# A slot table summed on two halves of TensorE, and the later expert tiles queued behind tile 0

## The chip, the cores and the metric

The kernel runs on one NeuronCore of a Trainium2 chip: TensorE (PE, with its weight loads shown as PEld), VectorE (DVE), ScalarE (ACT), GpSimd (POOL), SyncE (SP) and the DMA engines. The metric is the device time of one launch in microseconds; a time is the median of several executions.

## The reference, cut to what matters

The input `x` is 2 x 128 x 56 x 56 in fp32. Four layers each add their output to `x` after a normalisation: agent attention, a 3x3 convolution, a mixture of experts on 2x2 patches, and a two-way Mamba layer. The change is in the third:

```python
xp = patches of x                        # 1568 tokens of 512 numbers
probs = softmax(xp @ router_w)           # 8 experts
topv, topi = top_k(probs, 2)             # weights of the two, divided by their sum
for e in range(8):
    val, g = split(xp @ w1[e], 2)        # w1[e]: 512 x 2048
    out += gate[:, e] * ((val * sigmoid(g)) @ w2[e])   # w2[e]: 1024 x 512
```

## The kernel before, in words

The kernel does only the two chosen experts of each token. The 3136 choices (14 blocks of 112 tokens, two choices each) are sorted by expert into tiles of 128 slots, so that one tile belongs to one expert. There are at least 25 tiles (`self.fewest`); a `Switch` at the end runs the few more that the routing needs.

`PatchExperts.route` makes the plan. For each choice DVE computes tile and place in the tile. A table then has to say, for each tile (column) and each slot (row), which token sits there (`whom`) and with which weight (`share`). The table is a sum of 28 fp32 matmuls on PE, one for each block and choice (L1275): the stationary operand is `is_slot[:, t, :]`, 112 x 128, one where a token has that slot; the moving operand is `what[:, t]`, 112 x 64: 32 columns of token numbers, 32 of weights. All 28 add into one PSUM tile `inv` of 128 x 64, from which DVE copies `whom` (L1284) and `share` (L1286). The operands of the first choice lie in a buffer `room0` and those of the second in `room1`. These borrow one of the two buffers of the second weights (`w2`) and one of the two of the first weights (`w1`), so the second pair of weight reads waits until the last table matmul is done.

`PatchExperts.run` does the tiles. For a tile `j`:

- `expert(j)` loads the tile's expert number from SBUF into registers on SP (L1307), for the address of the reads;
- `up_weights` (L1314, 4 MB) and `down_weights` (L1319, 2 MB) read the expert's weights on SP's DMA queue, with two buffers each;
- `gather(j)` reads the tile's 128 token rows from DRAM with an indirect DMA on POOL (L1289), into one of four buffers `xr`;
- `up` transposes the rows on PE (four matmuls, L1331), copies them on DVE (L1333), makes 64 matmuls (L1342), a sigmoid on ACT (L1351) and a product on DVE (L1353);
- `down` of the tile before makes eight matmuls (L1359); ACT multiplies by the share (L1361) and writes the result to DRAM.

The program fixes the data and the order of the text; the order on each engine is made by a scheduler that puts work where its inputs are expected to be ready. In the program before, PE has the transposes of tiles 0 to 3 in front of tile 0's first L1342, and SP has thirteen expert numbers (L1307) in front of the first weight read.

fp32 matmuls stand in the trace as two records each.

Of the kernel before, what the change touches and what calls it, by code (L numbers as in the profile page):

```python
# [8 lines left out]
F32 = mybir.dt.float32  # L9
# [8 lines left out]
P = 128  # L18
# [995 lines left out]
class PatchExperts:  # L1014
# [15 lines left out]
    def route(self, dram, wpool, conv):  # L1030
# [9 lines left out]
        with tc.tile_pool(name="l2_route", bufs=1) as one, tc.tile_pool(  # L1040
# [10 lines left out]
            nc.gpsimd.dma_start(rw[:, :, :experts], a["L2_conv_router_w"].rearrange("(c q) e -> c q e", q=4))  # L1051
            four = one.tile([P, 32], F32, name="four")
            nc.vector.tensor_reduce(four, net.ident.rearrange("p (q e) -> p e q", q=4), AX.X, ALU.add)
            shape = [T, nt, experts]

            rank = one.tile([T, experts], F32, name="rank")
# [173 lines left out]


            self.slots = []
            inv = ps.tile([P, 512], F32, name="inv", tag="tr")
            rooms = [
                wpool.tile([P, self.hidden // P, 512], F32, name="room0", tag="w2").rearrange("p j d -> p (j d)"),
                wpool.tile([P, 4, 2 * self.hidden], F32, name="room1", tag="w1").rearrange("p q f -> p (q f)"),
# [1 line left out]
            for n, room in enumerate(rooms):  # L1238
                is_slot = room[:T, : nt * SLOTS].rearrange("t (n s) -> t n s", s=SLOTS)
                what = room[:T, nt * SLOTS : nt * (SLOTS + 2 * TILES)].rearrange("t (n h j) -> t n h j", h=2, j=TILES)  # L1240
                nc.vector.tensor_tensor(hots[n], hots[n], slot, ALU.mult)
                at = one.tile([T, nt], F32, name=f"at{n}")
                nc.vector.tensor_reduce(at, hots[n], AX.X, ALU.add)
                at_i = keep.tile([T, nt], I32, name=f"at_i{n}")
                nc.vector.tensor_copy(at_i, at)
                self.slots.append(at_i)
                tile_i = one.tile([T, nt], I32, name=f"tile_i{n}")
                nc.vector.tensor_single_scalar(tile_i, at_i, 7, ALU.logical_shift_right)
                tile_f = one.tile([T, nt], F32, name=f"tile_f{n}")
                nc.vector.tensor_copy(tile_f, tile_i)  # L1250
                low = one.tile([T, nt], F32, name=f"low{n}")
                nc.vector.scalar_tensor_tensor(low, tile_f, -float(SLOTS), at, ALU.mult, ALU.add)
                by_tile = [T, nt, TILES]
                nc.vector.tensor_tensor(
                    what[:, :, 0, :],
                    count_to[:T].unsqueeze(1).to_broadcast(by_tile),
                    tile_f.unsqueeze(2).to_broadcast(by_tile),
                    ALU.is_equal,
                )
                nc.vector.tensor_tensor(  # L1260
                    what[:, :, 1, :], what[:, :, 0, :], share[n].unsqueeze(2).to_broadcast(by_tile), ALU.mult
                )
                nc.vector.tensor_tensor(
                    what[:, :, 0, :], what[:, :, 0, :], token.unsqueeze(2).to_broadcast(by_tile), ALU.mult
                )
                for some in (range(per), range(per, nt)):
                    ts = slice(some[0], some[-1] + 1)
                    nc.vector.tensor_tensor(
                        is_slot[:, ts, :],
                        slot_of.unsqueeze(1).to_broadcast([T, per, SLOTS]),  # L1270
                        low[:, ts].unsqueeze(2).to_broadcast([T, per, SLOTS]),
                        ALU.is_equal,
                    )
                    for t in some:
                        nc.tensor.matmul(  # L1275
                            inv[:, : 2 * TILES],
                            is_slot[:, t, :],
                            what[:, t].rearrange("t h j -> t (h j)"),
                            start=n == 0 and t == 0,
                            stop=n == 1 and t == nt - 1,  # L1280
                        )

            self.whom = keep.tile([P, TILES], I32, name="whom")
            nc.vector.tensor_copy(self.whom, inv[:, :TILES])  # L1284
            self.share = keep.tile([P, TILES], F32, name="share")
# [12 lines left out]
    def run(self, wpool, work, ps):  # L1298
        net, nc, a = self.net, self.net.nc, self.net.a
        experts, hidden, toks = self.experts, self.hidden, self.toks  # L1300
        nj = hidden // P

        w1s = a["L2_conv_w1"].rearrange("e (c q) f -> e c q f", q=4)
        w2s = a["L2_conv_w2"].rearrange("e (j k) d -> e k j d", k=P)

        def expert(j):
            return bass.ds(nc.sync.value_load(self.whose[0:1, j : j + 1], min_val=0, max_val=experts - 1), 1)  # L1307

        ups = [wpool.tile([P, 4, 2 * hidden], F32, name="w1", tag="w1") for _ in range(2)]
        downs = [wpool.tile([P, nj, 512], F32, name="w2", tag="w2") for _ in range(2)]  # L1310

        def up_weights(j, e):
            w1 = ups[j % 2]
            nc.sync.dma_start(w1, w1s[e].rearrange("o c q f -> (o c) q f"))  # L1314
            return w1

        def down_weights(j, e):
            w2 = downs[j % 2]
            nc.sync.dma_start(w2, w2s[e].rearrange("o k j d -> (o k) j d"))  # L1319
            return w2  # L1320

        def gather(j):
            xr = work.tile([SLOTS, 512], F32, name="xr", tag="xr", bufs=4)
            self.rows_of(xr, self.xd, self.whom[:, j : j + 1], toks)
            return xr

        def up(j, w1, xr):

            tp = ps.tile([P, 512], F32, name="xr_ps", tag="tr")
            for q in range(4):  # L1330
                nc.tensor.transpose(tp[:, q * P : (q + 1) * P], xr[:, q * P : (q + 1) * P], net.ident)  # L1331
            xc = work.tile([P, 4, SLOTS], F32, name="xs_c", tag="xs_c")
            nc.vector.tensor_copy(xc.rearrange("c q s -> c (q s)"), tp)  # L1333
            ht = work.tile([P, nj, SLOTS], F32, name="ht", tag="ht")
            for c in range(2):
                parts = []
                for part in (1, 0):
                    h_ps = ps.tile([P, 512], F32, name="h_ps", tag="h", bufs=4)
                    for i in range(4):
                        f0 = part * hidden + (4 * c + i) * P  # L1340
                        for q in range(4):
                            nc.tensor.matmul(  # L1342
                                h_ps[:, i * SLOTS : (i + 1) * SLOTS],
                                w1[:, q, f0 : f0 + P],
                                xc[:, q, :],
                                start=q == 0,
                                stop=q == 3,
                            )
                    parts.append(h_ps)
                sg = work.tile([P, 4 * SLOTS], F32, name="sg", tag="sg")  # L1350
                nc.scalar.activation(sg, parts[0], AF.Sigmoid)  # L1351
                to = ht[:, 4 * c : 4 * c + 4, :].rearrange("k j s -> k (j s)")
                nc.vector.tensor_mul(to, parts[1], sg)  # L1353
            return ht

        def down(j, ht, w2):
            o_ps = ps.tile([P, 512], F32, name="o_ps", tag="o")
            for i in range(nj):
                nc.tensor.matmul(o_ps, ht[:, i, :], w2[:, i, :], start=i == 0, stop=i == nj - 1)  # L1359
            ot = work.tile([SLOTS, 512], F32, name="ot", tag="ot")  # L1360
            nc.scalar.mul(ot, o_ps, self.share[:, j : j + 1])  # L1361
            nc.scalar.dma_start(self.os[j * SLOTS : (j + 1) * SLOTS, :], ot)


        more = nc.values_load(self.more[0:1, 0:1], min_val=0, max_val=TILES - self.fewest)
        last = None
        for j in range(self.fewest):
            e = expert(j)
            w1, w2 = up_weights(j, e), down_weights(j, e)
            ht = up(j, w1, gather(j))  # L1370
            if last is not None:
                down(*last)
            last = (j, ht, w2)
        e0 = expert(self.fewest)
        first = up_weights(self.fewest, e0), down_weights(self.fewest, e0)
        xrs = {j: gather(j) for j in range(self.fewest, self.fewest + 3)}
        before = last
        for n in net.tc.Switch(more, TILES - self.fewest + 1):
            last = before
            for j in range(self.fewest, self.fewest + n):  # L1380
                if j == self.fewest:
                    w1, w2 = first
                else:
                    e = expert(j)
                    w1, w2 = up_weights(j, e), down_weights(j, e)
                ht = up(j, w1, xrs[j] if j in xrs else gather(j))
                down(*last)
                last = (j, ht, w2)
            down(*last)
# [759 lines left out]
```

## Time and profile before

| what | value |
|---|---|
| median of three timed runs | 3039.38 us (3038.12 to 3041.95) |
| the profiled execution, its own time | 3034.5 us |
| its span, first to last instruction | 3032.4 us |
| PE busy, share of the span | 2681.1 us (88%) |
| DVE busy | 2182.4 us (72%) |
| ACT busy | 1848.6 us (61%) |
| POOL busy | 1472.2 us (49%) |
| mean granted TensorE clock | 0.945 |
| L1342 (first expert product), PE | 407.4 us in 3584 records |
| L1359 (second expert product), PE | 201.2 us in 448 records |
| idle of POOL before L1289 | 519.0 us, 474.4 of it ended by PE `xr_ps` L1331 |

How to read it: busy times of engines overlap, so they do not add up to the span. A row `line engine op out<-in xcount | busy, mean ns | idle before <-releaser` names the line of the kernel, the engine, what is written and read, the count, and which event ended the idle time before. In the timeline a row is start, duration, engine, line, operands, count, and in brackets the idle time before it and what ended it. In a table of stretches each engine has its busy time and, in brackets, the number of its records; the last columns are the granted clock of TensorE as a share of full speed, the busy share of the DMA engines, and what they moved. SPq is the queue of SyncE.

### The profile page before, as it was taken

To read this page: it belongs to the slowest core of one execution; us is meant where nothing else is said; L and a number is where in the kernel's file an instruction comes from. 1 tells how busy PE (TensorE), PEld (TensorE's weight loads), DVE (VectorE), ACT (ScalarE), POOL (GpSimd) and SP (SyncE) were. 2 spreads that over 40 slices of the span, in tenths; PEclk is the share of its full clock that TensorE was granted. 3 is DMA by queue.
4 is the path that set the end of the run, shared out by engine and by line. 5 is a ranking of instruction groups with operands and counts; after the bars stand their busy time and mean duration, and the time that the engine had idled before them with its cause. 6 is when DMAs were issued, how large, how long until landed. Compare 5 with 4: busy or idle time off the path is not lost. (4 is left out here: it accounts for less than half of the span.)

```text
span 3032.4 us, 39344 instructions
## 1 busy us (share of the span) xinstructions
PE 2681.1 (88%) x14924; PEld 1275.2 (42%) x14924; DVE 2182.4 (72%) x1845; ACT 1848.6 (61%) x2942; POOL 1472.2 (49%) x801
## 2 busy tenths in 40 slices
PE   7999999999998799999997678888888888888874
PEld 3333333333335688787875323333323333233321
DVE  5978998999886300100101599999999999999996
ACT  5778788788751100000000488888888888888884
POOL 3000010010422100000001689999999999999995
PEclk9999999999999799999998899999998999999987
DMA  1000000000002768787874555566555565545560
GB/s 55 1 1 1 1 1 1 1 1 1 1 1 60 271 266 327 302 323 308 316 309 165 133 122 113 120 141 137 118 117 117 113 147 123 126 115 118 123 142 29
DMA packets 157931, 369.29 MB, mean 122 GB/s; under 512 B 25156, under 2 KB 114980, under 8 KB 154132
## 3 DMA queue, kind: packets, MB, share of 16 engines
q1 hardware_dynamic: 135744, 339.30, 38.7%
q0 software_dynamic: 5520, 15.62, 1.7%
q10 hardware_dynamic: 16452, 11.61, 1.2%
q8 instruction: 121, 1.98, 0.3%
q14 instruction: 94, 0.77, 0.1%
HBM read 297.89 MB, written 17.20 MB: 104 GB/s over the span
## 5 line engine op out<-in xcount | busy, mean ns | idle before, releaser
L1840 POOL TENSOR_TENSOR dBu<-dtu,Bs 128x896 f32<-128x896 f32 x448 | 943.1, 2150 | 18.0 <-DMA dtu<-sp_u 16.0
L1859 DVE TENSOR_TENSOR_SCAN h<-dA,dBu 128x896 f32<-128x896 f32 x448 | 883.9, 2009 | 28.9 <-ACT dA L1829 21.3
L620 ACT ACTIVATE ex<-sc 128x896 f32<-128x896 f32 (+1 forms) x700 | 602.6, 918 | 125.0 <-PE sc L617 113.7
L1881 PE MATMUL y<-h,both 128*64 128x448 f32 x1792 | 467.5, 614 | 99.5 <-POOL h L1868 93.5
L627 DVE TENSOR_TENSOR ex_sum<-ex_sum,ex 128x1792 f32<-128x1792 f32 (+1 forms) x238 | 492.5, 2069 | 35.3 <-ACT ex L620 21.3
L1342 PEld LDWEIGHTS h_ps<-xs_c,w 128*128 128x128 f32 x3584 | 403.7, 192 | 19.6 <-ACT ot L1361 17.7
L1342 PE MATMUL h_ps<-xs_c,w 128*128 128x128 f32 x3584 | 407.4, 276 | 0.0
L617 PE MATMUL sc<-q,k 32*128 32x448 f32 (+1 forms) x2800 | 403.8, 588 | 3.6 <-ACT ex L620 2.9
L1870 DVE TENSOR_TENSOR h<-h,c_ps 128x1792 f32<-128x1792 f32 (+1 forms) x168 | 326.5, 1944 | 31.9 <-ACT c_ps L1847 14.9
L1353 DVE TENSOR_TENSOR ht<-h_ps,sg 128x512 f32<-128x512 f32 x56 | 38.5, 691 | 418.0 <-PE h_ps L1342 365.8
L635 PE MATMUL av<-ex,va 128*32 128x448 f32 (+1 forms) x2800 | 334.4, 552 | 0.1
L582 POOL TENSOR_TENSOR a_e<-a_e,a_inv 112x784 f32<-112x784 f32 x14 | 41.6, 2973 | 584.1 <-ACT ex L620 394.5
L1829 ACT ACTIVATE dA<-dt,f_A 128x448 f32<-128x448 f32 x448 | 282.8, 636 | 57.1 <-DVE h L1859 41.2
L1829 ACT ACTIVATE dA<-dt,b_A 128x448 f32<-128x448 f32 x448 | 282.7, 635 | 30.0 <-DVE h L1859 21.2
L1289 POOL DMA_INDIRECT xr<-xd,whom x28 | 28.1, 1003 | 519.0 <-PE xr_ps L1331 474.4
L1881 PEld LDWEIGHTS y<-h,both 128*64 128x64 f32 x1792 | 119.1, 148 | 371.1 <-issue 208.9
L1868 POOL TENSOR_TENSOR h<-h,Cs 128x1792 f32<-128x1792 f32 (+1 forms) x70 | 253.3, 3619 | 2.9 <-PE sp_ps L1794 1.9
L617 PEld LDWEIGHTS sc<-q,k 32*128 32x128 f32 (+1 forms) x2800 | 137.8, 181 | 230.1 <-issue 132.5
L1351 ACT ACTIVATE sg<-h_ps 128x512 f32<-128x512 f32 x56 | 33.4, 597 | 308.8 <-PE h_ps L1342 301.5
L1359 PE MATMUL o_ps<-w,ht 128*128 128x512 f32 x448 | 201.2, 593 | 1.2 <-DVE ht L1353 1.2
L1361 ACT ACTIVATE ot<-o_ps,share 128x512 f32<-128x512 f32 x28 | 19.2, 687 | 244.0 <-PE o_ps L1359 244.0
L625 DVE TENSOR_TENSOR ex_sum<-ex 128x1792 f32<-128x1792 f32 x56 | 114.4, 2042 | 54.6 <-ACT ex L620 54.5
(332 smaller groups left out, 2980.9 us busy)
## 6 DMA issues: line engine op xcount, KB each, us to landing
w<-in_L_conv_w_dram SPq DMA_DIRECT2D x28, 4096.0 KB, 20.4
w<-in_L_conv_w_dram SPq DMA_DIRECT2D x28, 2048.0 KB, 10.7
Bs<-far SPq DMA_DIRECT2D x56, 896.0 KB, 8.0
Cs<-far SPq DMA_DIRECT2D x448, 112.0 KB, 3.0
dtu<-sp_u SPq DMA_DIRECT2D x108, 224.0 KB, 3.9
dt<-dt SPq DMA_DIRECT2D x108, 224.0 KB, 5.1
os<-ot ACTq DMA_DIRECT2D x28, 256.0 KB, 7.9
xd<-xt SPq DMA_DIRECT2D x14, 224.0 KB, 2.7
```

The costliest lines, as they stand in the source:

```text
L617: nc.tensor.matmul(sc[:size, j, :BLK], self.m.k[rows, at : at + size], self.q[rows, :], start=True, stop=True)
L620: nc.scalar.activation(ex[:size, 2 * g : 2 * g + 2, :], sc[:size, :, :BLK], AF.Exp, scale=scale)
L627: nc.vector.tensor_add(self.total[g][:size], self.total[g][:size], ex[:size])
L635: nc.tensor.matmul(self.av[rows, :BLK], self.m.va[:size, i, rows], self.ex[i][:size, h, :], start=i == 0, stop=i == STEPS - 1,)
L1342: nc.tensor.matmul(h_ps[:, i * SLOTS : (i + 1) * SLOTS], w1[:, q, f0 : f0 + P], xc[:, q, :], start=q == 0, stop=q == 3,)
L1359: nc.tensor.matmul(o_ps, ht[:, i, :], w2[:, i, :], start=i == 0, stop=i == nj - 1)
L1829: nc.scalar.activation(self.dA[u][:, r * BLK : (r + 1) * BLK], self.dt2[:, m, r, :], AF.Exp, scale=self.w.A[:, j, 2 * m + r : 2 * m + r + 1],)
L1840: nc.gpsimd.tensor_tensor(self.dBu[u], self.dtu2[:, m], self.B[:, j, :].unsqueeze(1).to_broadcast(shape), ALU.mult)
L1859: nc.vector.tensor_tensor_scan(hf, af, bf, 0.0, ALU.mult, ALU.add)
L1868: nc.gpsimd.tensor_tensor(h4, h4, self.C[j].unsqueeze(1).to_broadcast(shape), ALU.mult)
L1870: nc.vector.tensor_tensor(h4, h4, self.c_ps[:, :BLK].unsqueeze(1).to_broadcast(shape), ALU.mult)
L1881: nc.tensor.matmul(self.y[r * H : (r + 1) * H, m, :BLK], both, self.hc[j][:, m, r, :], start=False, stop=j == PAIRS - 1)
```

## The change

Two things are changed.

The slot table is summed the other way round. `what[:, t]` (64 columns) becomes the stationary operand and `is_slot[:, t, :]` (128 columns) streams. The result is the transposed table, 64 x 128. Blocks with an even number write it to PSUM partitions 0 to 63 and those with an odd number to 64 to 127, so each half of the array's columns has its own sum. One DVE copy (`table`) and one more matmul against `fold`, two identity blocks on top of each other, add the two halves and turn the table back; `whom` and `share` are copied as before. `fold` is made once by a DVE add.

In `run`, tiles 1 to 3 put whatever they have on PE in queue behind tile 0's first L1342 matmul, and each tile from 1 on puts what it has on SP (number loads, weight reads) behind an earlier `w1` read: tile 1 behind tile 0's, all later ones behind tile 1's. `issue_after` orders the queue only; it adds no wait for the other instruction's end. In the built program PE then has four transposes ahead of tile 0's L1342; the transposes of tiles 1, 2 and 3 each come after the L1342 group of the tile before. SP has two number loads ahead of the first weight read, one each ahead of the `w1` reads of tiles 1 and 2 and of the `w2` read of tile 2, and seven and six ahead of the `w2` reads of tiles 3 and 4. The order of ACT and POOL is the same.

```diff
+            fold = one.tile([P, 2 * TILES], F32, name="fold")
+            nc.vector.tensor_add(fold, net.ident[:, : P // 2], net.ident[:, P // 2 :])
...
-            inv = ps.tile([P, 512], F32, name="inv", tag="tr")
+            turned = ps.tile([P, 512], F32, name="turned", tag="tr")
...
                     for t in some:
+                        g = t % 2 * 2 * TILES
                         nc.tensor.matmul(
-                            inv[:, : 2 * TILES],
+                            turned[g : g + 2 * TILES, :SLOTS],
+                            what[:, t].rearrange("t h j -> t (h j)"),
                             is_slot[:, t, :],
-                            what[:, t].rearrange("t h j -> t (h j)"),
-                            start=n == 0 and t == 0,
-                            stop=n == 1 and t == nt - 1,
+                            start=n == 0 and t < 2,
+                            stop=n == 1 and t >= nt - 2,
                         )
 
+            table = one.tile([P, SLOTS], F32, name="table")
+            nc.vector.tensor_copy(table, turned[:, :SLOTS])
+            inv = ps.tile([P, 512], F32, name="inv", tag="tr")
+            nc.tensor.matmul(inv[:, : 2 * TILES], table, fold, start=True, stop=True)
...
+        starts, fetches = [], []
+
         def up_weights(j, e):
             w1 = ups[j % 2]
-            nc.sync.dma_start(w1, w1s[e].rearrange("o c q f -> (o c) q f"))
+            dma = nc.sync.dma_start(w1, w1s[e].rearrange("o c q f -> (o c) q f"))
+            fetches.append(dma.ins)
             return w1
...
-                            nc.tensor.matmul(
+                            mm = nc.tensor.matmul(
                                 h_ps[:, i * SLOTS : (i + 1) * SLOTS],
...
+                            starts.append(mm.ins)
...
         for j in range(self.fewest):
-            e = expert(j)
-            w1, w2 = up_weights(j, e), down_weights(j, e)
-            ht = up(j, w1, gather(j))
+            behind = ExitStack()
+            if 0 < j < 4:
+                behind.enter_context(net.tc.issue_after(starts[0]))
+            if j > 0:
+                behind.enter_context(net.tc.issue_after(fetches[min(j - 1, 1)]))
+            with behind:
+                e = expert(j)
+                w1, w2 = up_weights(j, e), down_weights(j, e)
+                ht = up(j, w1, gather(j))
             if last is not None:
                 down(*last)
             last = (j, ht, w2)
```

## The prediction

> **What bounds the kernel now.** I read the page's busy slices first (40 slices of 75.8 us), then busy time and clock by stretch, then the timeline of the hand-over from routing to experts.
>
> ```profile
> PE   7999999999998799999997678888888888888874
> DVE  5978998999886300100101599999999999999996
> ```
>
> Three regimes: attention and convolution (to slice 12), a stretch where only PE is full (slices 14 to 20, the experts), and the Mamba layer, where DVE and POOL are full. The change lies at the start of the second.
>
> ```profile
> core 0: us, PE busy (x) PEld busy (x) DVE busy (x) ACT busy (x) POOL busy (x), PEclk, DMA share, GB/s
> 1012.27:1015.68 3.41, 3.41 (x18) 3.41 (x18) 1.13 (x4) 0.00 (x0) 0.00 (x0) 0.50 1.08 384
> ...
> 1022.50:1025.90 3.40, 0.00 (x0) 0.00 (x0) 0.00 (x0) 0.00 (x0) 2.48 (x4) 0.50 0.88 309
> 1029.34:1032.75 3.41, 2.51 (x11) 1.74 (x10) 1.38 (x2) 0.00 (x0) 1.77 (x2) 0.50 1.17 458
> 1032.75:1036.16 3.41, 3.38 (x17) 3.00 (x16) 0.00 (x0) 0.00 (x0) 2.22 (x3) 0.50 0.98 422
> 1036.17:1039.00 2.83, 2.83 (x27) 2.83 (x27) 0.00 (x0) 0.08 (x1) 0.00 (x0) 1.00 1.01 424
> ...
> 1114.32:1592.70 478.38, 478.36 (x3252) 387.45 (x3252) 44.95 (x65) 40.70 (x65) 19.39 (x20) 1.00 0.80 313
> ```
>
> The last row decides what a saved microsecond is worth: from tile 4 to the last tiles PE is busy 478.36 of 478.38 us, so whatever tile 4 starts earlier, the whole rest starts earlier. The other rows show the hand-over: TensorE is idle at 1022 to 1026, and granted half its clock until 1036.16.
>
> ```profile
> 1008.87 12.18 PE L1275 MATMUL inv<-room 112*128 112x64 f32 x56 [3.29 <-DVE tile_f L1250]
> 1011.35 0.38 SPq L1314 DMA_DIRECT2D w<-in_L_conv_w_dram  x1
> 1021.08 0.19 DVE L1284 CAST whom<-inv 128x32 int32<-128x32 f32 x1 [7.62 <-PE inv L1275]
> 1021.56 1.13 POOL L1289 DMA_INDIRECT xr<-xd,whom  x1 [39.58 <-DVE share L1286]
> 1029.06 1.09 PE L1331 MATMUL xr_ps<-ident,xr 128*128 128x128 f32 x4 [8.01 <-DMA xr<-xd,whom]
> 1030.59 1.11 PE L1331 MATMUL xr_ps<-ident,xr 128*128 128x128 f32 x4 [0.45 <-DMA xr<-xd,whom]
> 1032.15 2.21 PE L1331 MATMUL xr_ps<-ident,xr 128*128 128x128 f32 x8 [0.45 <-DMA xr<-xd,whom]
> 1034.15 15.42 PE L1342 MATMUL h_ps<-xs_c,w 128*128 128x128 f32 x128
> ```
>
> This is the path: slot table (28 fp32 matmuls, each two records), `whom`, first gather, transposes of tiles 0 to 3 one after another as their gathers land, then tile 0's first product. The first weights, read at 1011.35, landed after 12.3 us, at 1023.7: not what is waited for.
>
> **What the Trainium skill says.** "TensorEngine Tiling (Array Packing)", Performance Considerations, advises swapping stationary and streaming operands plus 2x column tiling when the right-hand side is 64 wide or less. That is this edit, and the trace agrees that two 64-column halves run at once:
>
> ```profile
> L1881 PE MATMUL y<-h,both 128*64 128x448 f32 x8 | 1.7, 552 | 1.8 <-POOL h L1868 1.8
> ```
>
> Eight records of 448 columns in 1.7 us; whole-array L1359 steps every 0.44 us at 512 columns (16 records in 7.03), so eight of 448 would take 3.1 in a row. "TensorE: Matmul & The Clock Gate", Part 1, says the clock is halved after an idle window of about 3.4 us and restored after a busy one, in free-running windows. The trace agrees: the half-clock span 1005.4 to 1036.16 is nine times 3.41 us. It also shows that `inv`, busy throughout, did not restore the clock, while the stretch 1032.75 to 1036.16, full of transposes and L1342, did. "DMA: Bandwidth & Descriptors", Queues, rings and completion order, says each DMA engine takes turns between queues packet by packet. The gathers agree that the neighbour matters:
>
> ```profile
> xr<-xd,whom POOLq DMA_INDIRECT x1, 7.4
> ...
> xr<-xd,whom POOLq DMA_INDIRECT x1, 12.5
> ...
> g<-os,at_i POOLq DMA_INDIRECT x1, 3.3
> ```
>
> These are issue-to-landing times: 7.4 us for the gather of 1021.56, beside the 2 MB read `w2` (1011.99 to 1033.0); 12.5 us for that of 1030.41, mostly beside the 4 MB read `w1`; 3.3 us for one of the combine stage, beside no weights.
>
> **The change, part by part.**
>
> Slot table. A half-clock `inv` record takes 12.18/56 = 0.217 us, as long as an L1342 record at half clock (0.113 doubled) although only 64 columns stream: the 128-column weight load sets it (PEld 3.41 of 3.41). Afterwards 64 columns are loaded, 128 stream, and records of two halves overlap: 14 steps of about 0.215 per choice instead of 28. The second choice's operands come from DVE at 1012.69 (L1263). So: start 1008.87, 14 steps to 1011.9, wait, restart 1012.83, 14 steps and 0.2 drain: 1016.05 against 1021.05, -5.0. If the denser stream restores the clock by then, 14 steps of 0.113: 1014.6, -6.4. I give that one chance in three, as the gap at 1012 breaks most windows.
>
> The fold then adds a PSUM copy 128x128 (0.28, row L142), 0.03 of hand-over, and one matmul between two DVE steps: 0.63 for `tot` (L1172 ends 999.21, L1179 starts 999.84), 0.8 at half clock. Together 1.1, or 0.95. `whom` moves by -3.9 (cold) or -5.5 (warm), mean -4.4. `fold` itself is one DVE add of 0.2 (row L1522, same shape) at 913 us between small DVE steps; I charge 0.1, range 0 to 0.2.
>
> Order on PE. From landing of gather 0 (1028.92) to L1342 (1034.15) are 5.2 us. With tile 0's transposes alone: 0.13 hand-over, 1.09 transposes, 0.09 and 0.69 for L1333, 0.2 to L1342: 2.2, so -3.0. Twelve transposes come back later at full clock, 3 x 0.435 (1112.89 to 1113.32 for four): +1.3. Tile 1's copy L1333 hides under four L1359 products (4 x 0.86); tiles 2 and 3 have one product as cover, as tile 4 has already, with 0.14 left open: +0.3. Net -1.4. Gathers 5 to 7, formerly issued by 1035, now wait on POOL for transposes of tiles 1 to 3 (from 1043 on); they are needed from about 1130. Nothing else is queued behind them there.
>
> Clock. Tile 0 took 15.42 against 14.45 for later tiles: 0.97 lost in 2.0 cold microseconds, since the sixteen transposes had filled the window. Now PE idles about 8 us, does 1 us of transposes, waits 1 us, and must fill a window with L1342 itself. By the rows above, 2.51 busy of 3.41 was not enough and 3.38 was; taking 2.6 as the least, that is 2.6 to 6.0 us cold, mean 4.3, half of it lost: 2.15. Net +1.2 (0.3 to 2.0).
>
> Expert reads. SP had to load thirteen expert numbers ahead of the first read:
>
> ```profile
> L1307 SPq TENSOR_LOAD <-whose_i x13: 262/262/275, 1003.1 to 1009.9; - x13
> ```
>
> Pitch 6.8/12 = 0.56 us. Now two stand ahead: first `w1` 11 x 0.56 = 6.2 earlier, issued 1005.15, landing 1017.4. This earns nothing by itself (needed at 1027; unchanged it would land at 1023.7, still 3 us of cover). The second `w1` waits for the last slot-table matmul, which frees its buffer: 1016 instead of 1021.08. Until it lands, the remaining `w2`, four gathers and itself (about 7.3 MB) pass at some 0.39 MB/us (rows above: 309 to 458 GB/s): 1036; tile 1 asks at 1046. The moved loads (seven ahead of the fourth `w2`, 3.9 us) run while SP would wait for PE anyway: reads L1319 come 21 us apart.
>
> Gather 0. Issued 0.48 after `whom` starts, 1017.7 or 1016.0. Price taken: 7.4, since `w2` is again in flight (from about 1016 to 1026). Bounds 3.3 and 12.5; I add 0.2 for overrun.
>
> Sum at tile 4: -4.4 - 1.4 + 1.2 + 0.1 + 0.2 = **-4.3 us**. The profiled execution took 3034.5 (span 3032.4), so 3030.2 there. The timed runs stand 4.9 higher (median 3039.38); none of the steps depends on that, so 3035.1. About 0.2% (6.1 us) is what a measurement of this kernel can tell from no change; the forecast gain is below that.
>
> **The rivals.**
> 1. *The gather meets `w1` instead of `w2`* (ends slower). Because reads begin 6.2 us earlier and the table only 4 to 5, `w2` may be through before gather 0 moves; it then runs beside 4 MB of `w1`. For: 12.5 to 13.1 us for gathers 4 to 7. Against: at 1017.7 `w2` has only just begun, and needed 9.3 us beside gathers (1023.7 to 1033). Price +5.1: +0.8, 3040.2. From 11.7 us of landing time on, the gain is gone.
> 2. *The halves do not overlap*: 28 steps a choice as before, plus 1.1 for the fold. `whom` +1.1, total about +1.2, 3040.6. Against: L1881.
> 3. *More than forecast*: the table warms the clock (-5.5), tile 0 warms no later than before (1.2 back), and the gather needs 6.5: -5.5 - 1.4 + 0.1 - 0.9 = -7.7, 3031.7. For: windows may fall well; against: it takes all three.
>
> **How the numbers follow.** Forecast 0.68, rival 1 0.12, rival 2 0.06, rival 3 0.14. The forecast's own spread, cold to warm table and clock 0.3 to 2.0, is -6.5 to -2.5. The range 3031.0 to 3039.5 takes in rival 3 and the better half of rivals 1 and 2. Faster by over 0.2% needs below 3033.3: rival 3 and a quarter of the forecast, 0.31. Slower by over 0.2% is only a tail of rivals 1 and 2: 0.04. Same: 0.65.
>
> **What would show it.** Right: `turned` busy about 7 us instead of 12.2, its end near 1016; `whom` near 1017; first gather landing after 7 to 8 us; four, not sixteen, transposes ahead of L1342 at 1027; half clock to 1030 or 1031; tile 4 starting 4 to 5 us earlier, and the same shift at 1592. Wrong: `turned` still 12 us, a first gather over 9 us, L1342 idle for a `w` read, or a shift at tile 4 that is gone at the end.

## The result and the profile after

| | before | after |
|---|---|---|
| median of 20 runs | 3038.86 us (3034.71 to 3044.11) | 3033.20 us (3029.39 to 3048.44) |
| ratio of the medians, 95% interval | | 0.9983 (0.9975 to 0.9992) |
| the profiled execution, its own time | 3034.5 us | 3033.72 us |
| its span | 3032.4 us | 3031.7 us |
| PE busy | 2681.1 us | 2676.5 us |

The change gains some 5 us (by the interval 2.4 to 7.6). The spans of the two profiled executions show almost none of it, and the first thing to learn from the profile is why. The timeline of the hand-over, with the columns as before (the lines of the kernel have moved: the table is L1278, L1287 and L1289, the gather L1296, the transposes L1341, the first product L1352, its weight reads L1323 and L1329):

```profile
1004.69 0.37 SPq L1323 DMA_DIRECT2D w<-in_L_conv_w_dram  x1
1008.83 3.26 PE L1278 MATMUL turned<-room 112*64 112x128 f32 x28 [3.29 <-DVE tile_f L1252]
1012.70 1.75 PE L1278 MATMUL turned<-room 112*64 112x128 f32 x28 [0.62 <-DVE room L1265]
1014.50 0.29 DVE L1287 COPY table<-turned 128x128 f32<-128x128 f32 x1 [1.07 <-PE turned L1278]
1014.84 0.43 PE L1289 MATMUL inv<-fold,table 128*128 128x64 f32 x2 [0.39 <-DVE table L1287]
1015.32 0.19 DVE L1291 CAST whom<-inv 128x32 int32<-128x32 f32 x1 [0.53 <-PE inv L1289]
1015.80 1.13 POOL L1296 DMA_INDIRECT xr<-xd,whom  x1 [33.88 <-DVE share L1293]
1022.37 1.09 PE L1341 MATMUL xr_ps<-ident,xr 128*128 128x128 f32 x4 [7.09 <-DMA xr<-xd,whom]
1024.30 16.96 PE L1352 MATMUL h_ps<-xs_c,w 128*128 128x128 f32 x128 [0.84 <-DVE xs_c L1343]
1041.10 0.60 PE L1341 MATMUL xr_ps<-ident,xr 128*128 128x128 f32 x4
```

The reader sees each step of the change: the table in two bursts of 3.26 and 1.75 us where it was one of 12.18; copy and fold; `whom` 6.49 us after the first table matmul, formerly 12.21; one group of four transposes ahead of L1352, the next only behind it at 1041.10. Tile 0 starts 9.85 us earlier but takes 16.96 us instead of 15.42. By stretch of time, in the same columns as before:

```profile
1008.89:1012.31 3.42, 3.19 (x28) 2.79 (x28) 3.42 (x7) 0.00 (x0) 0.00 (x0) 0.50 0.98 422
1012.31:1015.72 3.41, 2.18 (x30) 1.81 (x30) 1.62 (x7) 0.00 (x0) 0.00 (x0) 1.00 1.09 461
1015.72:1019.13 3.41, 0.00 (x0) 0.00 (x0) 0.00 (x0) 0.00 (x0) 2.73 (x3) 1.00 0.85 321
1019.13:1022.55 3.42, 0.18 (x1) 0.21 (x2) 0.00 (x0) 0.00 (x0) 1.42 (x2) 0.50 1.07 367
1022.55:1025.96 3.41, 2.57 (x12) 2.17 (x12) 0.69 (x1) 0.00 (x0) 1.00 (x1) 0.50 1.10 410
1025.96:1029.37 3.41, 3.41 (x18) 3.41 (x18) 0.00 (x0) 0.00 (x0) 0.00 (x0) 0.50 1.07 455
1107.74:1586.20 478.46, 478.43 (x3252) 387.52 (x3252) 44.98 (x65) 40.70 (x65) 19.38 (x20) 1.00 0.80 313
```

The first row is one window of the clock in which the new table kept TensorE busy 3.19 us; after it the clock is full (second row) and the second choice runs at full speed. The idle third row costs the clock again, from 1019.13 to 1029.37. The last row is the yardstick of the prediction: tile 4 to the last tiles, 478.46 us, formerly 478.38 (the window after ends 0.08 us later, behind the start of the same transposes). Tile 4 started at 1114.32 and now starts at 1107.74, **6.58 us earlier**, and the combine stage's first gather moves by the same (1648.74 to 1642.18).

From there to the end of the span stand 1383.7 us before and 1389.5 us after, with the same instructions (PE 3704 records, DVE 806, in both). That stage took anything from 1378.5 to 1392.6 us in the thirteen profiles of this study, and in no order that follows the edits. So 5.8 of the 6.6 us won are hidden in this one pair of executions by a stage that differs for no reason shown here; only the medians show them.

The busy slices of the page:

```profile
PE   7999999999998799999996788888888888888874
DVE  5978998999887301010102589999999999999996
```

The hand-over lies in slice 13 (7 for PE in both kernels): 6 us of 75.8 are no whole digit there. What shows is the end of the experts in slice 21, where PE falls from 7 to 6, and the start of the Mamba layer in slices 22 and 23, where it rises from 6 and 7 to 7 and 8: everything there comes a little earlier.

### The profile page after: what moved, and what is told of

Its sections match the earlier page's. It is cut to its first block, busy times and chain, and to the rows that moved or that the text cites. A ratio compares the mean times of both kernels' runs of the same rounds, so it can differ in the third digit from the quotient of the medians.

```text
span 3031.7 us, 39354 instructions
## 1 busy us (share of the span) xinstructions
PE 2676.5 (88%) x14926; PEld 1269.6 (42%) x14926; DVE 2184.8 (72%) x1847; ACT 1849.2 (61%) x2942; POOL 1471.9 (49%) x801
## 3 DMA queue, kind: packets, MB, share of 16 engines
HBM read 297.89 MB, written 17.20 MB: 104 GB/s over the span
## 5 line engine op out<-in xcount | busy, mean ns | idle before, releaser
L1352 PEld LDWEIGHTS h_ps<-xs_c,w 128*128 128x128 f32 x3584 | 404.9, 193 | 21.5 <-ACT ot L1372 19.3
L1352 PE MATMUL h_ps<-xs_c,w 128*128 128x128 f32 x3584 | 409.1, 276 | 0.9 <-DVE xs_c L1343 0.8
L1296 POOL DMA_INDIRECT xr<-xd,whom x28 | 28.1, 1003 | 512.5 <-PE xr_ps L1341 474.9
```

What stands on the lines that cost most here:

```text
L1352: mm = nc.tensor.matmul(h_ps[:, i * SLOTS : (i + 1) * SLOTS], w1[:, q, f0 : f0 + P], xc[:, q, :], start=q == 0, stop=q == 3,)
```

## The experiments

Times of the end spread by some 15 us from run to run; the steps of the hand-over spread far less. There is one profile of each kernel, but steps that several kernels share can be compared: `whom` comes out within 0.02 us, and gather 0 within 0.6 us where the reads before it are the same (6.57, 6.82 and 7.16 in the changed kernel, e11 and e7). All runs are therefore read by the **distance from the first table matmul to tile 4's first product**: before 105.45 us, after 98.91. It may stand for the end, because from tile 4 to the first gather of the combine stage there are 534.36 to 534.44 us in all thirteen profiles. `whom` and "gather 0" are counted from the first table matmul and from the issue of the first gather (to its transposes on PE).

| kernel | table | PE order | SP order | whom | gather 0 | tile 0 takes | tile 4 | ratio to before (95%) |
|---|---|---|---|---|---|---|---|---|
| before | old | old | old | 12.21 | 7.50 | 15.42 | 105.45 | 1 |
| e1 | new | old | old | 6.49 | 8.61 | 15.51 | 102.05 | 0.9985 (0.9977 to 0.9993) |
| e3 | old | new | old | 12.22 | 7.13 | 17.20 | 105.44 | 1.0000 (0.9991 to 1.0009) |
| e4 | old | old | new | 12.22 | 12.35 | 15.85 | 111.80 | 1.0021 (1.0013 to 1.0029) |
| e2 | old | new | new | 12.22 | 12.63 | 16.21 | 109.94 | 1.0016 (1.0004 to 1.0028) |
| e9 | new | new | old | 6.48 | 8.65 | 15.98 | 100.00 | 0.9988 (0.9981 to 0.9996) |
| e11 | new | old | new | 6.49 | 6.82 | 15.89 | 108.24 | 1.0009 (0.9998 to 1.0020) |
| after | new | new | new | 6.49 | 6.57 | 16.96 | 98.91 | 0.9983 (0.9975 to 0.9992) |
| e5 | one half | new | new | 8.82 | 12.20 | 16.41 | 106.11 | 1.0003 (0.9992 to 1.0014) |
| e6 | new | new | new, `w2` first | 6.50 | 10.46 | 16.75 | 102.60 | 0.9986 (0.9978 to 0.9994) |
| e7 | new | new | new, PE kept busy | 6.49 | 7.16 | 14.56 | 96.63 | 0.9967 (0.9953 to 0.9981) |
| e8 | new | new | new, reads held | 6.49 | 3.54 | 16.72 | 95.64 | 0.9969 (0.9958 to 0.9980) |
| e10 | new | new | both of these | 6.49 | 3.58 | 14.56 | 92.96 | 0.9966 (0.9959 to 0.9973) |

The first eight rows are all combinations of the three parts. The gain or loss by the distance lies within the interval of the ratio in every row (of e10, at its edge). The parts do not add: table -3.40, PE order -0.01 and SP order +6.35 make +2.94, and together they give -6.54. Of the pairs, table and SP order come near their sum (+2.79 for +2.95, e11); the other two do not (-5.45 for -3.41, e9; +4.49 for +6.34, e2).

**e1, the table alone.** The changed kernel without both orders:

```diff
-            behind = ExitStack()
-            if 0 < j < 4:
-                behind.enter_context(net.tc.issue_after(starts[0]))
-            if j > 0:
-                behind.enter_context(net.tc.issue_after(fetches[min(j - 1, 1)]))
...
```

> Only the slot table is changed; the queues of PE and SP stay as before (sixteen transposes ahead of tile 0, thirteen number loads ahead of the first weight read). Both theories: the table ends near 1015.3 and the first gather is issued near 1015.8. Theory A, the parts add up (the sum of the prediction): the gather lands after 7.4 us, at 1023.2, the four transpose groups follow as before, tile 0's first product starts near 1028.5 and tile 4 near 1108.7, 5.6 earlier than before (1114.3). Theory B, the neighbour on the DMA engines decides: the first w1 read is still issued at 1011.3 and in flight until 1023.7, so the gather runs beside 4 MB of w1 and takes 12 to 13 us; it lands at 1028 or later, and the gain of the table is mostly gone: tile 4 between 1112 and 1116. Whole time: A -5 us, B within 2 us of before.

`whom` comes 5.7 us earlier, as in the changed kernel, but tile 4 only 3.40, between the values named. The first gather now takes 8.48 us to land, and those behind it 9.4 to 9.8: with the reads where they were, `w1` is in flight until 1024.58, while they run.

**e3, the PE order alone**, on the old table and the old reads:

```diff
             behind = ExitStack()
             if 0 < j < 4:
                 behind.enter_context(net.tc.issue_after(starts[0]))
```

> Only the PE order: tile 0's transposes alone ahead of its products; table and SP order as before. The gather meets w2 as before in both theories and lands after 7.4 us at 1028.9. Tile 0's first product then starts near 1031.1 instead of 1034.15 (-3.0); twelve transposes and two open copies come back (+1.6); the clock is cold longer, since nothing fills PE before tile 0 (tile 0 17.0 instead of 15.4: +1.5). Tile 4 between 1113.6 and 1114.8, whole time within 1 us of before. If the cold clock cost nothing, tile 4 would start at 1112.7.

Tile 0 starts 21.76 us after the table's first matmul instead of 25.28, so 3.5 are won; and from there to tile 4 it takes 83.68 instead of 80.17, so 3.5 are given back: tile 0 takes 17.20 us, 1.78 more, because the sixteen transposes no longer warm the clock for it, and the other 1.7 are the twelve transposes that come back between later products.

**e4, the SP order alone, and e2, both orders**, on the old table. e4 keeps only

```diff
             if j > 0:
                 behind.enter_context(net.tc.issue_after(fetches[min(j - 1, 1)]))
```

and e2 this and the line of e3.

> Only the SP order: two number loads ahead of the first weight read; table and PE order as before, so tile 0 waits for all four gathers. Theory A (reads that come earlier earn and cost nothing): gathers 7.4 to 7.7 us, tile 4 at 1114.3, no change. Theory B: w2 is through by 1023, the four gathers run beside the second w1 read; gathers 0 to 3 take 10 to 17 us (in the changed kernel the third and fourth took 14.1 and 17.2), the fourth lands near 1040, and tile 4 starts 5 to 9 us later than before; the whole is slower by as much.

> The table is summed as before; both queue orders (PE and SP) are those of the changed kernel. The table ends at 1021.05 and the first gather is issued at 1021.5. w1 and w2 of tile 0 start near 1004.7 and are through by about 1023. Theory A (parts add up): gather 7.4 us, tile 4 moves by -3.0 + 1.6 + 1.2 to 1.5 for the colder clock: 1114.1 to 1114.5, no change. Theory B (the neighbour decides): w2 is through when the gather moves, so it runs beside the second w1 read, takes 10 to 13 us, and tile 4 starts 3 to 6 us later than before, 1117 to 1120: slower in the whole by as much.

Both are slower, by 6.35 and 4.49 us at tile 4. The timeline of e2:

```profile
1005.64 0.42 SPq L1322 DMA_DIRECT2D w<-in_L_conv_w_dram  x1
...
1021.36 0.35 SPq L1316 DMA_DIRECT2D w<-in_L_conv_w_dram  x1
1021.85 1.13 POOL L1289 DMA_INDIRECT xr<-xd,whom  x1 [39.57 <-DVE share L1286]
...
1034.48 1.09 PE L1334 MATMUL xr_ps<-ident,xr 128*128 128x128 f32 x4 [13.15 <-DMA xr<-xd,whom]
```

and the DMA issues of e2, with the time to landing last (that `w2` with its `w1` of 1005.02, then the gather of 1021.85):

```profile
w<-in_L_conv_w_dram SPq DMA_DIRECT2D x1, 4096.0 KB, 12.2
w<-in_L_conv_w_dram SPq DMA_DIRECT2D x1, 2048.0 KB, 17.1
...
xr<-xd,whom POOLq DMA_INDIRECT x1, 12.5
```

`w2`, issued at 1005.64, is through 17.1 us later, at 1022.8, when the gather has only begun; the next 4 MB `w1` is queued from 1021.36. The gather runs beside it and needs 12.5 us. This is rival 1, with its mechanism and its price (+5.1 forecast), on a table that is 5.7 us later than the changed one.

**e9, table and PE order**, that is the changed kernel without the two lines of e4.

> The changed kernel without its order on SP: the new slot table and the PE order stay, the first w1 is read some 6.5 us later again. Distances are counted from the first table matmul to tile 4's first product: 105.45 before, 98.91 after, 102.05 with the table alone. Theory A (the prediction's sentence that the earlier reads earn nothing by themselves): the first gather lands after 6.5 to 7.4 us as after, tile 4 at 98.9 to 99.5, median as after. Theory B (the order decides which read the gather meets): w1 is then still in flight until about 1024.5 as in the run with the table alone, so gather 0 lands after 8 to 9 us and tile 4 comes at 100.5 to 101.5; by the median 1.5 to 2.5 us above the changed kernel. If the table and the PE order already gave the whole gain, B fails; if tile 4 comes at 102 or more, the PE order earns nothing with the new table either.

```profile
xr<-xd,whom POOLq DMA_INDIRECT x1, 8.5
```

The gather's landing (8.51) is that of theory B: `w1` was read from 1012.11 to 1024.84, and the gather landed at 1025.10. Tile 4 at 100.00 is between both theories: tile 0 starts 0.4 us after the beginning of a window of the clock (1026.77 to 1030.18), is cold for 3.0 us and not for 5.1, and takes 15.98 us, not 16.96. So with the new table and the PE order the SP order earns 1.1 us at tile 4 (2.1 on the gather, less 1.0 on the clock). That is not far above the 0.6 us by which the gather differs between profiles, and the medians can't tell these two kernels apart.

**e11, table and SP order**, the changed kernel without the line of e3.

> The changed kernel without its order on PE: the new slot table and the order of reads on SP stay, and the sixteen transposes of tiles 0 to 3 stand ahead of tile 0's first product again. Distance from the first table matmul to tile 4's first product: 98.91 with all three parts, 102.05 with the table alone, 100.00 with table and PE order. Theory A (the PE order is worth the same with or without the read order, about 2 us with the new table): 101 to 102. Theory B (the parts depend on each other through the gathers): gathers 2 and 3 then land as late as in the changed kernel, after 14 and 17 us beside the second w1, at 24 to 28 us after the first table matmul; PE waits in order for all four, tile 0's first product starts 29 to 30 us after it instead of 15.5, and tile 4 comes at 109 to 111, later than before (105.45) by some 5 us. The median then lies 3 to 6 us above the kernel before; with A it lies 3 to 4 us below.

```profile
1022.30 1.09 PE L1341 MATMUL xr_ps<-ident,xr 128*128 128x128 f32 x4 [7.34 <-DMA xr<-xd,whom]
1023.96 1.11 PE L1341 MATMUL xr_ps<-ident,xr 128*128 128x128 f32 x4 [0.57 <-DMA xr<-xd,whom]
1030.74 1.08 PE L1341 MATMUL xr_ps<-ident,xr 128*128 128x128 f32 x4 [5.66 <-DMA xr<-xd,whom]
1035.23 1.08 PE L1341 MATMUL xr_ps<-ident,xr 128*128 128x128 f32 x4 [3.41 <-DMA xr<-xd,whom]
1036.11 14.11 PE L1352 MATMUL h_ps<-xs_c,w 128*128 128x128 f32 x112
```

Theory B's mechanism, at 0.8 us less than its lower end. Gathers 0 and 1 pass beside `w2`, 2 and 3 fall behind the second `w1`, and PE waits for them in order although the rows of tile 0 were there at 1022.2. Tile 0 starts at 27.60 instead of 15.47. In the changed kernel the same gathers are as late (the answers for the third and fourth, issued at 1018.55 and 1019.86):

```profile
xr<-xd,whom POOLq DMA_INDIRECT x1, 14.1
...
xr<-xd,whom POOLq DMA_INDIRECT x1, 17.2
```

but nobody waits: tile 2 is transposed at 1062.69. With the new table the PE order is worth 9.3 us beside the SP order and 2.05 without it (e1 to e9); on the old table 1.86 beside the SP order (e4 to e2) and nothing without it (e3).

**e5, one half.** Operands are exchanged as in the change, but all blocks add into the same 64 partitions, so that nothing runs side by side:

```diff
-                        g = t % 2 * 2 * TILES
+                        g = 0
...
-                            start=n == 0 and t < 2,
-                            stop=n == 1 and t >= nt - 2,
+                            start=n == 0 and t == 0,
+                            stop=n == 1 and t == nt - 1,
```

> The changed kernel, but all 28 table matmuls write to partitions 0 to 63, so no two of them can overlap; the fold then takes 64 rows instead of 128. Times counted from the table's first matmul; tile 4 stands at 105.4 in the kernel before and 98.9 in the changed one. Theory A (the gain of the table is the overlap of the halves): table busy about 12 us as before at half clock, or about 9 if the denser stream brings the full clock after the first stretch; whom 8.5 to 13.3 after the start instead of 6.5. With w1 and w2 long in flight the gather then runs partly beside the second w1 read: 8 to 12.5 us. Tile 4 at 103 to 110. Theory C (the gain comes from the swap alone, the shorter weight load): table under 7.5 us, tile 4 near 99.

```profile
1008.84 7.98 PE L1278 MATMUL turned<-room 112*64 112x128 f32 x56 [3.29 <-DVE tile_f L1252]
...
1030.34 1.09 PE L1343 MATMUL xr_ps<-ident,xr 128*128 128x128 f32 x4 [12.72 <-DMA xr<-xd,whom]
```

The table takes 7.98 us, not 12.18. The exchange alone saves 4.2 us, and it does so through the clock: until 1012.29 a record starts every 0.21 us in both kernels, then the clock is full here and one starts every 0.11 us, while it stays at half in the kernel before. Whether the 64 columns fewer to load or the 64 more to stream restore it is not separated. The two halves, in which theory A saw the gain of the table, bring the last 2.33 us of `whom` (8.82 to 6.49). And these decide the end: at 1018.14 the gather is 2.3 us later than in the changed kernel, `w2` is through at 1022.67, and the gather needs 12.20 us instead of 6.57. So 2.33 us on the table are worth 7.20 at tile 4 (106.11 to 98.91).

**e6, `w2` ahead of `w1`** for tile 0, so that the gather meets the large read. In the edit `seconds` collects the `w2` reads as `fetches` does the `w1` reads:

```diff
-                w1, w2 = up_weights(j, e), down_weights(j, e)
+                if j == 0:
+                    w2 = down_weights(j, e)
+                    with net.tc.issue_after(seconds[0]):
+                        w1 = up_weights(j, e)
+                else:
+                    w1, w2 = up_weights(j, e), down_weights(j, e)
```

> The changed kernel with tile 0's reads the other way round: the 2 MB w2 first, then the 4 MB w1. Gather 0 is issued at the same place (6.9 after the table's first matmul) but now meets w1 for its whole way; tile 0 needs w1, which lands some 8 us later than w2 does in the changed kernel. Theory B (the neighbour decides): the gather takes 10 to 13 us instead of 6.4, tile 4 at 102.5 to 105.5 instead of 98.9. Theory A (the gather costs 7 us beside any read): it takes 6.4 to 7.5 us and tile 4 stays at 99 to 100, unless tile 0 waits for w1 itself, which would show as its first product starting later than the copy of its rows.

```profile
1016.71 1.13 POOL L1296 DMA_INDIRECT xr<-xd,whom  x1 [33.90 <-DVE share L1293]
...
1027.17 1.08 PE L1342 MATMUL xr_ps<-ident,xr 128*128 128x128 f32 x4 [10.98 <-DMA xr<-xd,whom]
```

The table is that of the changed kernel, and the second pair of reads is issued as there, after the last table matmul. The gather takes 10.46 us instead of 6.57, and tile 4 comes 3.69 us later. The neighbour of the gather is a cost by itself; the medians of the two kernels don't tell them apart.

**e7, PE kept busy.** Seven idle fp32 matmuls of 512 columns behind the fold; tile 0 is ordered behind them:

```diff
+            idle = ps.tile([P, 512], F32, name="idle", tag="tr")
+            for _ in range(7):
+                with tc.issue_after(mm.ins):
+                    mm = nc.tensor.matmul(idle, table, net.x[:, 0, :512], start=True, stop=True)
+            self.filled = mm.ins
...
+            if j == 0:
+                behind.enter_context(net.tc.issue_after(self.filled))
```

> The changed kernel with seven more matmuls of 128 x 512 after the fold, whose result nobody reads, to keep TensorE busy while the gather is under way (6.0 us at full clock). Cold-clock theory: the clock stays at full through tile 0, whose products take 14.5 instead of 17.0 us: tile 4 at 96.0 to 96.6 after the table's first matmul instead of 98.9, whole time 2.5 us less than the changed kernel (about -8 us against before). Rival: the pauses around the four transposes (about 2 us in all) still halve the clock, or the added matmuls run into the arrival of the gather: tile 4 at 98.5 to 99.5, nothing gained.

```profile
1015.86 6.23 PE L1293 MATMUL idle<-x,table 128*128 128x512 f32 x14
...
1023.70 0.63 PE L1346 MATMUL xr_ps<-ident,xr 128*128 128x128 f32 x4 [1.61 <-DMA xr<-xd,whom]
...
1025.16 14.56 PE L1357 MATMUL h_ps<-xs_c,w 128*128 128x128 f32 x128 [0.84 <-DVE xs_c L1348]
```

The clock stays full: tile 0 takes 14.56 us, and tile 4 comes 2.28 us earlier than in the changed kernel, though the gather took 0.6 us longer. So the idle wait costs some 2.9 us through the clock: 2.40 on tile 0 and 0.47 from the start of its transposes to its first product.

**e8, reads held.** Only the first `w1` is read ahead of the gathers. A copy of one element from the gathered rows into `w2`'s buffer (whose value the read then overwrites) makes the first `w2` wait until gather 0 has landed, and SP's next reads are ordered behind it:

```diff
+            if j == 1:
+                behind.enter_context(net.tc.issue_after(seconds[0]))
...
-                w1, w2 = up_weights(j, e), down_weights(j, e)
-                ht = up(j, w1, gather(j))
+                w1, xr = up_weights(j, e), gather(j)
+                if j == 0:
+                    nc.scalar.copy(downs[0][0:1, 0, 0:1], xr[0:1, 0:1])
+                w2 = down_weights(j, e)
+                ht = up(j, w1, xr)
```

> The changed kernel with tile 0's w2 read (and with it all later weight reads) held back until gather 0 has landed: one element of its buffer is first written from the gathered rows by ACT. Only the first w1 read is in flight when the gather is issued, and it is nearly through. Theory B (the neighbour decides): the gather takes 3.5 to 5 us instead of 6.4, tile 0 starts 1.5 to 3 us earlier; the later reads (6.3 MB and three gathers, issued about 11 after the table's start, some 18 us) are there before tile 1 asks for w1 about 33 after the start. Tile 4 at 96 to 97.5. Theory A: the gather stays at 6.4, tile 4 at 99. Rival for the worse: tile 1 or tile 0's second product waits for the held reads, visible as PE idle before L1353 of tile 1, tile 4 later than 99.

```profile
1016.50 1.14 POOL L1296 DMA_INDIRECT xr<-xd,whom  x1 [33.86 <-DVE share L1293]
...
1020.04 1.08 PE L1342 MATMUL xr_ps<-ident,xr 128*128 128x128 f32 x4 [4.06 <-DMA xr<-xd,whom]
```

Gather 0 now moves with no weight read beside it, and its transposes start 3.54 us after its issue; tile 4 comes 3.27 us earlier than in the changed kernel, at 95.64, a little below the 96 to 97.5 named. The held `w2` lands at 1032.3, in time for tile 0's second product at 1038.96.

**e10, both**, with four idle matmuls, since the gather lands sooner.

> The changed kernel with both additions: the first w2 and all later reads held until gather 0 has landed (alone: distance from the first table matmul to tile 4's first product 95.64), and four idle fp32 matmuls of 512 columns behind the fold, which keep TensorE busy from 1015.9 to 1019.4 (seven of them alone: 96.63). The result of the idle matmuls is not used. If the gather's neighbour and the clock are two separate costs, their savings add: 98.91 - 3.27 - 2.28 = 93.4, gather 0 lands in 3.4 us, tile 0 takes 14.5 us at full clock, and the median is 5 to 6 us below the changed kernel's, near 3027. If they are the same cost (an earlier gather only exposes the cold clock, or the warm clock only helps because the gather is late), it is 95.5 to 96.5 and the median no lower than that of either alone.

```profile
1014.27 3.65 PE L1293 MATMUL idle<-x,table 128*128 128x512 f32 x8
1014.95 1.13 POOL L1301 DMA_INDIRECT xr<-xd,whom  x1 [33.87 <-DVE share L1298]
...
1018.53 0.63 PE L1347 MATMUL xr_ps<-ident,xr 128*128 128x128 f32 x4 [0.61 <-DMA xr<-xd,whom]
1018.68 0.42 SPq L1334 DMA_DIRECT2D w<-in_L_conv_w_dram  x1
...
1019.99 14.56 PE L1358 MATMUL h_ps<-xs_c,w 128*128 128x128 f32 x128 [0.84 <-DVE xs_c L1349]
```

The two savings add: 92.96 against 93.4 expected, 5.95 us ahead of the changed kernel and 12.5 ahead of the one before. The median is 3028.16 us (21 runs). Its interval, 0.9959 to 0.9973, lies below that of the changed kernel, so this version beats both; that it beats e7 and e8 is shown by the distance only.

## Why the prediction was right or wrong

Right: the sign, the path and the size within what the medians tell. -4.3 us was forecast for tile 4 and the end, and a median of 3035.1 us; it is 3033.20. The trace has -6.58 at tile 4, half as much again as the forecast, and the interval of the medians (-7.6 to -2.4) is wide enough to hold both. The prediction took 0.2% (6.1 us) as the least that can be told from no change; with 20 runs of each kernel the interval is 0.08% to either side and excludes no change. Step by step, in us:

| step | forecast | trace |
|---|---|---|
| `fold`'s add, start of the table | +0.1 | -0.04 |
| table and fold, to `whom` | -4.4 (-3.9 cold, -5.5 warm) | -5.72 |
| gather 0 | +0.2 | -0.93 |
| transposes of tile 0 alone | -3.0 | -3.16 |
| colder clock in tile 0 | +1.2 | +1.54 |
| transposes and copies back | +1.6 | +1.73 |
| sum at tile 4 | -4.3 | -6.58 |

The first row can't be read to a tenth: the table starts anywhere from 1007.7 to 1010.2 us in the thirteen profiles. The misses that count are the table (1.3 us) and the gather (1.1), and both lie on the same side.

- **Table.** The step that was mis-sized is the weight of one in three for the warm case. Warm came, and not by luck: in all nine profiles with the exchanged operands (e5 included) the clock is restored 3.3 to 3.5 us after the first table matmul. The sub-steps held: -6.56 for the matmuls (warm -6.4 forecast), fold and copy +0.84 (0.95 forecast for the warm case). The sentence that the gap at 1012 breaks most windows is what failed: the window that counts ended at 1012.31, and the gap (1012.09 to 1012.70) took only its last 0.22 us.
- **Gather.** 6.44 us to landing where 7.4 was taken, between the bounds. Rival 3 had 6.5 for it; with two of the three things that rival 3 needed (warm table, quicker gather) and not the third (tile 0 paid for the clock), its sum corrected by +1.2 is -6.5.
- **PE order and clock.** Right to 0.3 us together, and e3 shows that on the old table they cancel: what the order wins, the clock and the returning transposes take. In the changed kernel the three rows add to +0.11; the order earns its place by what tile 0 no longer waits for (e11). Tile 0 was cold from 1024.30 to 1029.37; half of that is 2.5, and 16.96 less 14.45 is 2.51.
- **Expert reads.** "This earns nothing by itself" is the sentence that fell. Moving the reads decides which transfer the gathers meet. It costs 6.35 us on the old table (e4), 4.50 there beside the PE order (e3 to e2) and 6.19 on the new table without the PE order (e1 to e11); it earns 1.1 us only where both other parts are in place (e9). The prediction asked only when weights are needed, and treated the meeting as a risk of the whole change; its sign depends on the two other parts. So the sum of the steps holds for the three parts together, and not for the table or the SP order alone.
- **Rivals.** Rival 1 is real, and this change is 2.3 us away from it (e5). Here the prediction had luck: it held a cold table, with `whom` 3.9 us earlier, twice as likely as a warm one. That is 8.3 us after the table's first matmul, and in e5, with 8.82, the gather met `w1` and the gain was gone (+0.66 at tile 4). By this, an estimate, the forecast would have failed in the case that it held more likely. Rival 2, as a mechanism, doesn't happen: 28 matmuls of two records took 5.0 us of busy time on two halves and 7.98 on one (e5). Its price was wrong too: without the overlap `whom` would still come 3.39 us earlier, not 1.1 later. It is the gather that would take the gain.
- **Marks named beforehand.** Four transposes ahead of L1352, half clock to 1029.37 (1030 to 1031 named), and the same shift at tile 4 and at the end of the experts (1592.70 to 1586.12) are as named. `turned` busy 5.0 us and not 7, L1352 at 1024.30 and not 1027, and 6.58 where 4 to 5 stood, all follow from the first two steps.

What stays open is the 14 us by which the Mamba stage differs between executions of the same instructions; no run was made for it.

## What to carry to other kernels

When an early transfer is moved earlier still, ask what small transfer on the path it will meet, and check the answer against the new start of that transfer, not the old one: the same two lines were 6.35 us of loss on the old table, 6.19 on the new one with the old PE order, and 1.1 us of gain with all parts. Three edits at one hand-over are priced together, since each moves what the next one collides with. Where one saved microsecond lies ahead of a stage that spreads by ten, read a distance that ends before that stage, and use the medians only to confirm it.

## What the runs showed of the hardware

- The price of an indirect gather of 256 KB follows from its neighbour. From issue to landing it took 3.4 us alone (e10, where `w1` was through 1.3 us after the issue), 6.4 to 7.4 beside a 2 MB read (the changed kernel, e3, the kernel before), 8.5 to 12.5 beside a 4 MB read (e1, e9, e4, e2), and 17.2 as the fourth in a row there. The Trainium skill, "DMA: Bandwidth & Descriptors", Queues, rings and completion order, explains a dependence on the neighbour by queues that take turns by packets, and the packets in the traces agree. In e2, from 1026.5 to 1033.3 us beside `w1`, the weights' queue moved 80 packets with 2.62 MB and the gathers' queue 75 packets with 0.27 MB. In the changed kernel, from 1020.2 to 1021.6 us beside `w2`, it was 147 packets with 0.30 MB and 80 packets with 0.27 MB. So a packet of `w1` carries 32 KB and one of `w2` 2 KB, and the same 0.27 MB of gathered rows took 6.8 us beside the large packets and 1.4 us beside the small ones. No run changed the packets alone, so that they are the cause is argued, not shown.
- The wait before the first packet is another part of the price, and it does not tell the two reads apart: for 4.3 us after the issue of gather 0 the gathers' queue moved nothing in the changed kernel (beside `w2`) and in e1 (beside `w1`); in e10 it was 1.8 us. So what counts is what is in flight some 4 us after the issue: in e5 `w2` still had 4.5 us to go at the issue of gather 0, and the gather needed 12.20 us to its transposes, as beside `w1`. In e1 and e9 the gather landed within 0.3 us of the end of `w1`, which had some 8 us to go at the issue, and `w2` followed on that queue; in e6 the second `w1` followed, and the gather needed 10.46 us to its transposes.
- A row that is busy 3.41 of 3.41 us need not warm the clock. 64 streamed columns behind 128 loaded ones (the old table) left it at half for the whole 12.18 us; 128 streamed columns behind 64 loaded ones, with a record every 0.21 us as before and no overlap (e5), restored it 3.45 us after the first record.
- The Trainium skill, "TensorE: Matmul & The Clock Gate", Part 1, calls the windows free-running, so that the point of change varies. Here it hardly did: half clock set in 3.3 to 3.5 us before the first table matmul in all thirteen profiles, although the table itself starts anywhere within 2.5 us. The measurement decides for this kernel; what ties the windows to the program is open.
